# An edge network on one core: the node layer's own-row product moved into the product stage, and a hand-ordered head

## The chip, the cores and the metric

The kernel runs on one core of a Trainium2 chip. The core has a matrix engine (PE, with its weight loads shown as PEld), a vector engine (DVE), an activation engine (ACT), a general engine (POOL, GpSimd) and a queue engine (SP) that only issues transfers. Transfers are issued by SP, ACT and POOL and carried out by 16 DMA engines. Each engine works through its own list of instructions in order; semaphores tie the lists together. The metric is device time in microseconds; lower is better. The profile is one execution of the same program.

## The reference

One layer of a graph network over 12,500 nodes with 64 features and 212,500 edges, sorted by destination, with a hidden width of 128:

```
h   = relu(layernorm(x))                                  # 12500 x 64
e   = silu([h[src], h[dst], w] @ eW1 + eb1)               # 212500 x 128, eW1 is 129 x 128
e   = silu(e @ eW2 + eb2)                                 # 212500 x 128
agg = segment_sum(e, src, 12500)                          # 12500 x 128
out = x + silu([h, agg] @ nW1 + nb1) @ nW2 + nb2          # nW1 is 192 x 128, nW2 is 128 x 64
```

So the edges arrive sorted by destination, and their results must be summed by source.

## The kernel before, in words

The first edge layer is split: `h @ eW1[:64]` (table `ta`, by source) and `h @ eW1[64:128]` (table `tb`, by destination) are made once per node. Each table entry is kept as a rounded value and the rest that rounding left, two times 128 numbers.

**Head.** Constants, the source list `srcR`, the destination list `dstR`, the edge weights `ewR` and the first 16 x 128 nodes (`x0`) are loaded; `norm` normalises the nodes, `first_rows` makes a small `tb0`, and `tb00` from its first 512 nodes, so that edges can be handled before all of `tb` exists. `destinations` turns `dstR` into `rowsD`, `sources` turns a half of `srcR` into bucket (`bkt`) and place in the bucket (`locE`), `edge_weights` splits `ewR` into a rounded part and a rest and writes both to DRAM (`ews`).

**Sends.** Edges are handled in 208 blocks of 1024. For a block, `load` fetches the window of `tb` rows that its destinations need, `count` (DVE: `oh`, `each`, `pick`, `terms`, `rank`, `to`) computes the row of the scratch table `q` that each edge goes to, and `send` multiplies the window by a selection (`qp`, L493), copies it out (`qs`, ACT, L505 and L508) and scatters 128 edges with one indirect transfer on POOL (L515), eight for a block and 1,661 in all. `send_all` interleaves the pieces of `send(s)` and `count(s+1)`, three pieces for a block.

**Product stage.** A generator `feed` makes `ta` and `tb` in the pauses between pieces: for every 4 of the 100 node buckets, `products` transposes the normalised nodes (`ht`, L721), calls `product` for `ta`, stores the transposed nodes to `hd`, and calls `product` for `tb`. `product` does four matmuls (L246), two ACT copies that round (L250) and two DVE subtractions that form the rest (L253). Every `yield` in these generators is a point at which the order of issue goes over to something else.

**Steps.** The edges of a source bucket come back from `q` in 14 levels (`LEVELS`) of 25 batches; 450 steps of 512 edges do `pt`, `e1`, `p2`, `e2` and the segment sum `seg`. Which sends come between which steps is fixed when the program is written, by `PLAN_*` and `marks`. A level can be fetched (`fetch`) once its last block has been sent.

**Node layer.** In the last level each of the 25 batches is followed by `nodes`: two matmuls of `aggT` with `w1g` (L312), two of the nodes read back from `hd` with `w1n` (L315), SiLU (L317), a second product (L321), the sum with `x` (L324, `os`), and two stores on SP (L126). `nodes_in` loads `xr` (two transfers, L126 too) and the transposed nodes (L302). A flag that says whether the general path is needed is computed at the very end (L980 to L984).

The four engine lists PE, DVE, ACT and SP are in written order from the allocation of the PSUM pools on; before that a scheduler orders them. The granted clock of PE is shown in each window.

Of the kernel before, what the change touches and what calls it, by code (L numbers as in the profile page):

```python
# [28 lines left out]
F32 = mybir.dt.float32  # L29
# [10 lines left out]
P = 128  # L40
L = 125
# [38 lines left out]
def tile_gnn(ctx: ExitStack, tc: tile.TileContext, x, src, dst, ew, eW1, eb1, eW2, eb2, nW1, nb1, nW2, nb2, out):  # L80
# [11 lines left out]

    const = ctx.enter_context(tc.tile_pool(name="const", bufs=1))
# [35 lines left out]
    NE, EARLY, FIRST_PAIRS = 16, 30, 2  # L129
# [11 lines left out]
    firstR = lp.tile([P, NT], I32, name="firstR")  # L141
# [4 lines left out]
    nc.vector.memset(srcR[96:NP, LAST:], N)  # L146
    nc.vector.memset(ewR[96:NP, LAST:], 0.0)
    nc.vector.memset(firstR, 0)
    for a in range(2):
        nc.vector.memset(dstR[a * HB + HB // 2 : (a + 1) * HB, NT - 1], (2 + a) * STEP)  # L150
    ones = const.tile([1, P], F32, name="ones")
    nc.vector.memset(ones, 1.0)
    warm = const.tile([1, 1], F32, name="warm")
    nc.scalar.activation(warm, ones[:, 0:1], AF.Sqrt)
    for j0, j1 in ((0, G), (G, NE)):
        nc.sync.dma_start(x0[:, j0:j1], x[j0 * P : j1 * P, :].rearrange("(p j) d -> p j d", j=j1 - j0))
    vec = lambda v, lo_, n, m: bass.AP(tensor=v.tensor, offset=v.offset + lo_, ap=[[m, n], [1, m]])
    three = lp.tile([3, H], F32, name="three")
    three2 = lp.tile([3, 2, H], F32, name="three2")
    nc.scalar.dma_start(three[0:2, :], rows_of(eW1[2 * D : 2 * D + 1, :], 2))  # L160
    nc.scalar.dma_start(three[2:3, :], rows_of(eb1, 1))
    for to, v, queue in ((srcR, src, nc.sync), (ewR, ew, nc.scalar)):
        for p0, p1 in ((0, 96), (96, NP - 1)):
            queue.dma_start(to[p0:p1, :], vec(v, p0 * PAIR, p1 - p0, PAIR))
        queue.dma_start(to[NP - 1 : NP, :LAST], vec(v, (NP - 1) * PAIR, 1, LAST))
    shown = lambda p0, n, lo_, dims: bass.AP(tensor=dst.tensor, offset=dst.offset + p0 * PAIR + lo_, ap=[[PAIR, n]] + dims)
    MORE = LAST - BLK - HALF
    for T in range(NT):
        for a in range(2):
            whole = min(HB, NP - T * HB) - (a == 1 and T == NT - 1)  # L170
            for n0, n1 in ((0, HB // 2), (HB // 2, HB)):
                n1 = min(n1, whole)
                of = shown(T * HB + n0, n1 - n0, a * HALF, [[BLK, 2], [1, HALF]])
                nc.sync.dma_start(dstR[a * HB + n0 : a * HB + n1, T], of)
            n = min(HB, NP - T * HB)
            nc.scalar.dma_start(firstR[a * HB : a * HB + n, T : T + 1], shown(T * HB, n, 0, [[1, 1]]))
    at = HB + NP - 1 - (NT - 1) * HB
    nc.sync.dma_start(dstR[at : at + 1, NT - 1, 0], shown(NP - 1, 1, HALF, [[1, HALF]]))
    nc.sync.dma_start(dstR[at : at + 1, NT - 1, 1, :MORE], shown(NP - 1, 1, BLK + HALF, [[1, MORE]]))
    last = bass.AP(tensor=dst.tensor, offset=dst.offset + E - FEW, ap=[[PAD, 1], [0, PAD // FEW], [1, FEW]])  # L180
    nc.scalar.dma_start(dstR[at : at + 1, NT - 1, 1, MORE:].rearrange("p (r e) -> p r e", e=FEW), last)

    ident = const.tile([P, P], F32, name="ident")
    make_identity(nc, ident)
    identb = const.tile([P, P], BF16, name="identb")
    nc.vector.tensor_copy(identb, ident)
    part_i = const.tile([P, 1], I32, name="part_i")
    nc.gpsimd.iota(part_i, pattern=[[0, 1]], base=0, channel_multiplier=1)
    part = const.tile([P, 1], F32, name="part")
    nc.vector.tensor_copy(part, part_i)  # L190
    part1 = const.tile([P, 1], F32, name="part1")
    nc.vector.tensor_scalar(part1, part, 1.0, None, op0=OP.add)
    nodes_i = const.tile([P, L], I32, name="nodes_i")
    nc.gpsimd.iota(nodes_i, pattern=[[1, L]], base=1, channel_multiplier=0)
    nodes1 = const.tile([P, L], F32, name="nodes1")
    nc.vector.tensor_copy(nodes1, nodes_i)
# [4 lines left out]
    for a in range(2):  # L201
        half = slice(a * D, (a + 1) * D)
        nc.gpsimd.dma_start(w1[half, :, :], eW1[: 2 * D, :].rearrange("(s k) f -> k s f", s=2))
    same = const.tile([P, 1], F32, name="same")
# [9 lines left out]
    for extra in extras:  # L214
        nc.vector.tensor_copy(extra, plus[:, :, None].to_broadcast([P, 2, HALF]))
# [8 lines left out]
    none = const.tile([P, NB], BF16, name="none")  # L224
    nc.vector.memset(none, 0.0)
    bad = const.tile([P, 2], F32, name="bad")
    nc.vector.memset(bad, 0.0)

# [9 lines left out]
    def product(s, hr, ps, tag, to):  # L238

        abs_ = []  # L240
        for a in range(2):

            half = slice(a * D, (a + 1) * D)
            ab = ps.tile([P, G // 2, H], F32, name="ab", tag=tag)
            for i in range(G // 2):
                nc.tensor.matmul(ab[:, i], hr[half, i, :], w1[half, s, :], start=True, stop=True)  # L246
            abs_.append(ab)
# [3 lines left out]
        yield  # L251
        for a in range(2):
            nc.vector.tensor_tensor(to[:, a, 1], abs_[a], to[:, a, 0], op=OP.subtract)  # L253

    hd = dram.tile([P, NB // 2, P], F32, name="hd")
# [3 lines left out]
    NW = 3  # L259
    wins = [const.tile([P, 2, 2, 2, H], F32, name=f"win{i}") for i in range(NW)]  # L260
    sels = [const.tile([P, P], BF16, name=f"sel{i}") for i in range(NW)]
    for win in wins:
        nc.vector.memset(win, 0.0)
# [71 lines left out]
    with ExitStack() as work:  # L335
# [67 lines left out]
        def count(s):  # L403
# [37 lines left out]
            if s:  # L441
                picked()
# [677 lines left out]
```

## Time and profile before

| | us |
|---|---|
| median of 3 runs (2364.10 to 2369.81) | 2369.58 |
| the profiled execution, time | 2367.31 |
| the profiled execution, span | 2365.5 |
| first and last indirect send on POOL start | 42.16 and 2173.3 |
| busy: PE, DVE, POOL, ACT | 2028.7, 1814.7, 1655.9, 1333.0 |

Rows of the timeline have start, duration, engine, line and operation; "x8" is the number of instructions merged into the row, and the bracket is the idle time of the engine ahead of it with what ended it. Rows of the windows give the busy time of PE, PEld, DVE, ACT and POOL in a stretch, with the number of instructions, then the granted clock of PE (1.00 is full speed), the share of the DMA engines and GB/s. In the source view three durations are least, median and most, in ns.

### The profile page before, as it was taken

What the parts mean: (1) busy time and instruction counts of PE and PEld (TensorE: products, weight loads), DVE (VectorE), ACT (ScalarE), POOL (GpSimd) and SP (SyncE); (2) the same over time, 40 slices, a digit from 0 to 9 for tenths busy, and PEclk for the clock granted to TensorE, in tenths of its full rate; (3) what the DMA queues carried; (4) which work ended last, traced back from release to release, by engine and by line L of the source; (5) the groups of instructions that cost most, each with busy time, mean ns of one, the idle gap of its engine ahead of it and who ended that gap; (6) DMA issues with size and microseconds to landing.
All of it is one profiled execution on the core that took longest, in us unless ns stands there. A gap on an engine that the chain in (4) does not pass through costs nothing.

```text
span 2365.5 us, 47589 instructions
## 1 busy us (share of the span) xinstructions
PE 2028.7 (86%) x16818; PEld 1902.7 (80%) x16818; DVE 1814.7 (77%) x2865; ACT 1333.0 (56%) x2966; POOL 1655.9 (70%) x1724
## 2 busy tenths in 40 slices
PE   4667798952599779969995999999999999989997
PEld 2455697942499669959995999999999999989885
DVE  8899788885488868886886888888888888875221
ACT  3334464631277547737773777666666666656542
POOL 5777777777777777777777777777777777776110
PEclk9655597965699879979996999999999999999998
DMA  5566797964488647867884888888888888878662
GB/s 161 188 235 231 268 298 248 324 225 133 155 297 263 224 170 250 264 197 255 288 286 143 284 280 265 268 276 271 285 267 291 274 275 277 272 244 277 196 196 85
DMA packets 239835, 572.83 MB, mean 242 GB/s; under 512 B 46756, under 2 KB 99072, under 8 KB 239177
## 3 DMA queue, kind: packets, MB, share of 16 engines
q1 hardware_dynamic: 155283, 390.76, 51.5%
q0 software_dynamic: 54112, 124.65, 14.4%
q10 hardware_dynamic: 30196, 54.31, 7.3%
q8 instruction: 136, 2.23, 0.4%
q14 instruction: 108, 0.88, 0.1%
HBM read 356.61 MB, written 212.87 MB: 241 GB/s over the span
## 4 chain that ended last, share of the span: by engine, by line
PE 58%; DMA 12%; DVE 11%; POOL 6%; issue 4%; ACT 2%; SPq 2%; POOLq 0%; DVEq 0%; ACTq 0%
PE seg L675 15%; PE p L661 14%; PE pt L622 10%; DMA q<-qs,to 8%; PE pt L615 6%; POOL q L515 6%; PE qp L493 6%; PE lr L601 4%; DMA out_dram<-os 3%; DVE each L434 1%; DVE oh L426 1%; PE bc L379 1%; DVE rank L453 1%; DVE terms L451 1%; DVE pick L415 1%
## 5 line engine op out<-in xcount | busy, mean ns | idle before, releaser
L515 POOL DMA_INDIRECT q<-qs,to x1661 | 1616.1, 973 | 526.5 <-issue 396.9
L631 ACT ACTIVATE e<-pt 128x512 f32<-128x512 f32 x450 | 268.7, 597 | 496.2 <-PE pt L622 495.2
L675 PE MATMUL seg<-one,e 128*128 128x125 f32 x3600 | 502.3, 283 | 2.0 <-DVE aggT L686 1.7
L661 PE MATMUL p<-w,e 128*128 128x128 f32 x3600 | 498.6, 282 | 0.0
L661 PEld LDWEIGHTS p<-w,e 128*128 128x128 f32 x3600 | 449.9, 195 | 9.9 <-issue 9.2
L675 PEld LDWEIGHTS seg<-one,e 128*128 128x128 f32 x3600 | 444.2, 193 | 9.4 <-issue 4.9
L622 PE MATMUL pt<-oneT,a 125*128 125x128 f32 (+1 forms) x2800 | 423.0, 289 | 14.4 <-DMA a<-ta 8.5
L493 PEld LDWEIGHTS qp<-win,pick 128*128 128x128 f32 x1664 | 268.5, 224 | 202.6 <-ACT qs L505 121.6
L493 PE MATMUL qp<-win,pick 128*128 128x256 f32 x1664 | 347.7, 340 | 93.5 <-ACT qs L505 60.6
L505 ACT COPY qs<-qp 128x512 f32<-128x512 f32 x418 | 245.1, 587 | 323.9 <-DMA q<-qs,to 222.9
L622 PEld LDWEIGHTS pt<-oneT,a 125*128 125x128 f32 x2800 | 356.8, 194 | 18.3 <-issue 9.7
L644 DVE TENSOR_TENSOR one<-misc,qt 128x500 f32<-128x500 f32 x450 | 302.4, 672 | 78.1 <-PE seg L675 42.1
L686 DVE TENSOR_TENSOR aggT<-aggT,seg 128x500 f32<-128x500 f32 x325 | 218.4, 672 | 185.9 <-PE seg L675 182.2
L434 DVE TENSOR_REDUCE each<-oh 128x100 bf16<-128x800 bf16 x208 | 321.0, 1543 | 7.2
L615 PE MATMUL pt<-ident,qt 128*128 128x128 f32 x1800 | 276.3, 277 | 10.4 <-ACT qs L505 10.1
L606 ACT CAST oneT<-lr 125x512 fp32r<-125x512 f32 x450 | 265.5, 590 | 13.2 <-PE lr L601 13.2
L665 ACT ACTIVATE e<-p 128x512 f32<-128x512 f32 x450 | 268.7, 597 | 6.1 <-PE p L661 6.1
L655 ACT COPY p<-b2f 128x512 f32<-128x512 f32 x450 | 267.2, 594 | 0.0
L451 DVE TENSOR_TENSOR terms<-oh,misc 128x800 f32<-128x800 bf16 x208 | 203.6, 979 | 38.2 <-PE misc L439 38.2
L615 PEld LDWEIGHTS pt<-ident,qt 128*128 128x128 f32 x1800 | 215.3, 144 | 19.7 <-ACT qs L505 11.0
L453 DVE TENSOR_REDUCE rank<-terms 128x8 f32<-128x864 f32 x208 | 219.0, 1053 | 7.2
L426 DVE TENSOR_TENSOR oh<-misc,bkt 128x800 bf16<-128x800 f32 (+1 forms) x209 | 203.8, 975 | 2.4 <-ACT bkt L831 2.4
(153 smaller groups left out, 1653.4 us busy)
## 6 DMA issues: line engine op xcount, KB each, us to landing
a<-ta SPq DMA_DIRECT2D x350, 512.0 KB
qt<-q SPq DMA_DIRECT2D x250, 288.0 KB
qt<-q SPq DMA_DIRECT2D x100, 576.0 KB
q<-zeros ACTq DMA_DIRECT2D x25, 1080.0 KB
q<-qs,to POOLq DMA_INDIRECT x1661
win<-tb SPq DMA_DIRECT2D x208, 120.0 KB
tb<-got SPq DMA_DIRECT2D x30, 512.0 KB
q<-zeros ACTq DMA_DIRECT2D x20, 720.0 KB
```

Source lines behind the costliest of these rows:

```text
L434: nc.vector.tensor_reduce(each, oh.rearrange("p t b -> p b t"), AX.X, OP.add)
L493: nc.tensor.matmul(qp[:, t % 2, :k], halves(pick[:, t * P : (t + 1) * P]), halves(win[:, :k, v]), start=v == 0, stop=v == 1,)
L515: ins = nc.gpsimd.indirect_dma_start(out=q[:], out_offset=bass.IndirectOffsetOnAxis(ap=to[:k, j : j + 1], axis=0), in_=qs[:k, t % 2, a, :] ...
L606: nc.scalar.copy(halves(oneT), st[k].pop("lr"))
L615: nc.tensor.matmul(pt[:, t, :], qt[:, j, :H], ident, is_transpose=True, start=t == 0, stop=False, skip_group_check=True)
L622: nc.tensor.matmul(pt[:, cols, :], halves(a[:L, b, i * H : (i + 1) * H]), halves(oneT[:, cols, :]), start=False, stop=i == 1, skip_group_c ...
L631: nc.scalar.activation(e1, pt, AF.Silu)
L644: nc.vector.tensor_tensor(one.rearrange("p (b j) l -> p b j l", j=n), spots[:, None, None, :].to_broadcast(wide), loc[:, tiles[0][1] : til ...
L655: nc.scalar.copy(p2, b2f)
L661: nc.tensor.matmul(p2[:, t, :], e1[:, t, :], w2, start=False, stop=t == G - 1, skip_group_check=True)
L665: nc.scalar.activation(e2, p2, AF.Silu)
L675: nc.tensor.matmul(item[2][:, b, :], e2[:, t, :], one[:, t, :], start=j < G, stop=j >= G * (n - 1))
```

## The change

Three things are done at once.

1. **`product`.** The rest is no longer subtracted on DVE. PE multiplies the rounded copy with a negated identity (`less`) into the same PSUM tile, and ACT copies what is left. The `yield` inside `product` goes, so the calls are plain.
2. **The node layer's own rows.** `products` multiplies the transposed nodes with `w1n` at once (two matmuls `zo`, two ACT copies) and stores 128 x 500 numbers to `own` in place of 128 x 256 to `hd`. In the last level one matmul with `w1g` over 500 columns is added to what DVE has copied from `own` into a PSUM bank, and one SiLU follows. The copy for the next batch is issued right behind `os` (`then`). The last level's first fetch comes one batch later.
3. **The head.** All four lists are in written order from the start. Only 512 nodes, the first half of the destination list (by rows) and of the source list (by columns) and the first block's weights are loaded ahead of the first window; everything else goes on the SP queue behind it, the small weights too, which POOL issued before. The memsets move from DVE to POOL. `FIRST_PAIRS` is 3. All of `send(0)` comes ahead of the feed, and the feed gives nothing in the first three pieces. The flag is computed with the last block (`flagged`), and the order of the last steps is written out (`ending`).

The order of issue on PE from the first step to the last sends, 13,329 instructions, is the same in both kernels. In the product stage the old order puts 50 products into the 20 blocks 3 to 22 (blocks counted by their `bc` matmul, L379); the new one puts 48 products, 23 pairs of transposes and 24 pairs of `zo` matmuls into the 15 blocks 5 to 19, and none behind.

```diff
@@ product
             for i in range(G // 2):
-                nc.tensor.matmul(ab[:, i], hr[half, i, :], w1[half, s, :], start=True, stop=True)
+                nc.tensor.matmul(
+                    ab[:, i], hr[half, i, :], w1[half, s, :], start=i == 0, stop=False, skip_group_check=True
+                )
...
             nc.scalar.copy(halves(to[:, a, 0]), abs_[a])
-        yield
         for a in range(2):
-            nc.vector.tensor_tensor(to[:, a, 1], abs_[a], to[:, a, 0], op=OP.subtract)
+            nc.tensor.matmul(
+                abs_[a], halves(less), halves(to[:, a, 0]), start=False, stop=True, skip_group_check=True
+            )
+        for a in range(2):
+            nc.scalar.copy(halves(to[:, a, 1]), abs_[a])
@@ products
-            yield from product(0, hr, mm, "mm", rows_a)
-            nc.sync.dma_start(hd[:, b // 2 : (b + G) // 2, :], hr)
-            yield
+            product(0, hr, mm, "mm", rows_a)
+            zos = fp1.tile([P, G * L], F32, name=f"zos{b // G % 2}")
+            zo = [mm.tile([P, G // 2, L], F32, name="zo", tag="mm") for _ in range(2)]
+            for a in range(2):
+                half = slice(a * D, (a + 1) * D)
+                nc.tensor.matmul(zo[a], w1n[half, :], hr[half, :, :L], start=True, stop=True)
+            for a in range(2):
+                nc.scalar.copy(zos.rearrange("p (i a l) -> p i a l", a=2, l=L)[:, :, a], zo[a])
+            yield
+            nc.sync.dma_start(own[:, b // G, :], zos)
...
-            yield from product(1, hr, mm, "mm", got)
+            product(1, hr, mm, "mm", got)
@@ nodes, nodes_in
-        hr = sb.tile([P, G // 2, P], F32, name="hrn")
-        nc.sync.dma_start(hr, hd[:, b // 2 : b // 2 + G // 2, :])
+        zo = sb.tile([P, G * L], F32, name="zo")
+        nc.sync.dma_start(zo, own[:, B, :])
...
+        if bank is not None:
+            nc.tensor.matmul(bank, w1g, sums, start=False, stop=True, skip_group_check=True)
+            nc.scalar.activation(zsv, bank, AF.Silu, bias=nb1c)
...
         nc.vector.tensor_tensor(os_, o, xr, op=OP.add)
+        for more in then:
+            nc.vector.tensor_copy(bank, more())
         yield
@@ send_all
+                if s == 0:
+                    for _ in send(s):
+                        pass
+                for j, _ in enumerate(itertools.zip_longest(send(s) if s else (), count(s + 1))):
                     if s + 1 == nblocks and j == 1:
                         counted(s)
+                        flagged()
@@ s_pt
-                fetch(c * (NB // G) + B + NQ)
+                i = c * (NB // G) + B
+                while len(fetched) <= i + NQ and (len(fetched) < final or i + 3 >= final):
+                    fetched.append(0)
+                    fetch(len(fetched) - 1)
@@ the head
-            order = [rows_, rows_, made[0], src0, made[0], src0, weights, lists_, made[0], made[0], src0, src0, lists_]
-            order += [lists_, src0, src0]
+            order = [rows_, lists_, rows_, firstw, lists_, src0, rows_, made[0], src0, firstw, lists_, made[0], src0]
+            order += [lists_, made[0], lists_]
             for part_ in order:
                 next(part_)
+            nc.vector.tensor_copy(upto, zone)
             load(0)
             load_rows(0)
+            load(1, rows=False)
+            load_sources(1)
+            load_weights()
+            for _ in src0:
+                pass
+            for _ in count(0):
+                pass
+            load_destinations(1)
+            load_x0(G, NE)
...
             for win in wins[1:]:
-                last_rows_of(win)
+                last_rows_of(win, nc.sync)
             later_weights()
...
+            feed = itertools.chain(norm(x0[:, G:], NE - G), turns(made[1:], 2), destinations(1))
+            feed = itertools.chain(feed, itertools.islice(rest, 40), checks(), rest)
             for i, _ in enumerate(send_all(0, 2 * FIRST)):
+                if i == 0:
+                    nc.scalar.copy(halves(ewH), ewR)
-                for _ in range(2 if i < PIECES else 4):
+                for _ in range(0 if i < PIECES else 2 if i < 2 * PIECES else 4):
                     next(feed, None)
```

More of the change, by code (lines that the diff above doesn't have):

```diff
@@ L258, in tile_gnn, with last_rows_of @@
     base_i = const.tile([1, NT * HB], I32, name="base_i")
[L259 to L263, printed above, removed]
-    def last_rows_of(win):
+    def last_rows_of(win, queue):
         for a in range(2):
```

323 lines of the change are left out of this document (168 added, 155 removed).

## The prediction

> **What bounds the kernel now.** I read the page's costliest groups first, then the source view and the timeline of the scatter on POOL, then windows by stage, then the chain of waits at the end.
>
> ```profile
> span 2365.5 us, 47589 instructions
> L515 POOL DMA_INDIRECT q<-qs,to x1661 | 1616.1, 973 | 526.5 <-issue 396.9
> ```
>
> ```profile
> L515 POOL DMA_INDIRECT q<-qs,to x1661: 905/969/1905, 42.2 to 2173.3; - x185
> ```
>
> ```profile
> 42.16 1.91 POOL L515 DMA_INDIRECT q<-qs,to  x1 [10.50 <-ACT qs L508]
> ...
> 92.30 0.96 POOL L515 DMA_INDIRECT q<-qs,to  x1 [2.98 <-ACT qs L508]
> ...
> 126.13 0.96 POOL L515 DMA_INDIRECT q<-qs,to  x1 [2.73 <-ACT got L250]
> ...
> 1000.06 0.97 POOL L515 DMA_INDIRECT q<-qs,to  x1 [0.30 <-issue]
> 1001.33 0.97 POOL L515 DMA_INDIRECT q<-qs,to  x1 [0.30 <-issue]
> ```
>
> ```profile
> 78.00:240.00 162.00, 117.65 (x539) 88.44 (x537) 149.58 (x267) 63.93 (x185) 119.75 (x121) 0.51 0.64 228
> ...
> 400.00:1500.00 1100.00, 915.30 (x7724) 872.42 (x7723) 850.66 (x1298) 635.93 (x1405) 836.73 (x864) 0.88 0.72 240
> 1500.00:2174.00 674.00, 658.44 (x6046) 646.23 (x6045) 571.27 (x880) 438.43 (x959) 513.04 (x529) 1.00 0.85 274
> 2174.00:2365.00 191.00, 170.94 (x1367) 149.54 (x1365) 47.25 (x87) 85.17 (x170) 18.47 (x26) 0.97 0.55 167
> ```
>
> POOL's scatter is the pace of the whole middle. Two neighbours start 1.27 us apart (1000.06, 1001.33): 0.97 of work and 0.30 of issue. The window 400 to 1500 holds 864 of them, 1100/864 = 1.273 each; from 126.13, where the 57th starts, to 2173.3 there are 1604 intervals, 1.276 each. So POOL has no slack after 126 us: whatever delays the stream there arrives at the end in full, and whatever starts it earlier does too. Ahead of it are 42.16 us of head and, up to 126.13, stalls of 83.97 - 56 x 1.273 = 12.7 us (3.0 of them at 92.30). A block of eight sends has 8 x 1.273 = 10.2 us.
>
> In the product stage (78 to 240) PE is 73% busy at a granted clock of 0.51, and DVE is 92% busy. Behind the last send the node layer takes 191 us.
>
> ```profile
> 2229.80 0.43 DVE os L324
> 2230.25 0.32 SPq L126
> 2230.62 0.40 SPq L126
> ...
> 2232.46 3.42 DMA out_dram<-os
> 2236.09 0.44 DVE os L324
> ```
>
> This chain repeats for 18 batches at about 6.3 us: `os` frees the buffer that SP's next `xr` load waits for, SP goes on to the store of an older batch, and that store's landing frees the buffer of the next `os`. PE is not in it.
>
> **The change part by part.**
>
> The rows for the product stage:
>
> ```profile
> 210.29 0.65 PE L379 MATMUL bc<-rowsD,sel 128*128 128x512 bf16 x1
> ...
> 213.46 1.22 PE L493 MATMUL qp<-win,pick 128*128 128x256 f32 x4 [0.46 <-ACT hr L725]
> ...
> 226.17 0.37 ACT L725 COPY hr<-ht 128x256 f32<-128x256 f32 x1 [1.81 <-PE ht L721]
> 226.60 2.24 PE L246 MATMUL ab<-w,hr 64*128 64x128 f32 x16 [0.46 <-ACT hr L725]
> 227.90 0.65 ACT L250 CAST rows_a<-ab 128x256 fp32r<-128x256 f32 x2 [1.35 <-PE ab L246]
> ...
> 231.68 0.69 PE L721 MATMUL ht<-ident,xs 128*128 128x128 f32 x2 [0.22 <-ACT qs L505]
> ```
>
> ```profile
> L253 DVE TENSOR_TENSOR got<-ab,got x58: 402/415/431, 24.3 to 272.4; 128x256 f32<-128x256 f32 x58
> ...
> L253 DVE TENSOR_TENSOR rows_a<-ab,rows_a x50: 406/415/426, 70.0 to 259.2; 128x256 f32<-128x256 f32 x50
> ```
>
> ```profile
> 1702.87 0.69 PE L493 MATMUL qp<-win,pick 128*128 128x256 f32 x4
> ...
> 2201.68 0.69 PE L315 MATMUL z<-hrn,w1n 64*128 64x250 f32 x4
> ...
> 2353.48 0.37 PE L981 MATMUL fp<-ident,s 128*1 128x128 f32 x1 [0.57 <-DVE os L324]
> ...
> 2354.27 0.14 DVE L984 CAST flag_i<-m 1x1 int32<-1x1 f32 x1
> ```
>
> *Product.* DVE loses 108 x 0.415 = 45 us; that is work beside POOL, worth nothing by itself. PE gains two matmuls a product and, because they stand right behind the four and read what ACT has copied, a wait in the middle. Before, two products run back to back in 2.24, 1.12 each. After, from the start of the four: ACT begins 1.30 later (226.60 to 227.90), its first copy ends at 1.67, the first `less` starts at about 1.72; the second copy ends at 1.95, the second `less` runs 2.0 to 2.26 (a 128x256 matmul by the `qp` row is 1.22/4 = 0.30 with its tail). So 2.26 us of PE's list instead of 1.12. Bounds: 1.72 if the wait were hidden (1.12 + 2 x 0.30), 2.9 if ACT is busy with another copy pair (+0.65) whenever it is wanted. I take 2.26: nothing stands between the matmuls, and ACT has room (64 us busy in 162). ACT gains two copies of 0.37 a product.
>
> *Own rows.* Two `zo` matmuls a group have the shape of L315, 0.69 at full clock; at the half clock of this stage `qp` takes 1.22 (213.46) where it takes 0.69 at full clock (1702.87), so I take 1.15 (bounds 1.0 and 1.4) and 0.65 of ACT.
>
> *Their place.* The order now has 48 products, 24 `zo` pairs and 23 transpose pairs in 15 blocks. PE for these: base 15 x 3.5 (two `qp` of 1.22, `bc` 0.65, two small counts 0.4) = 52; 48 x 2.26 = 108; 24 x 1.15 = 28; 23 x 0.65 = 15; the `b2f` fill 4. Sum 207 us, 13.8 a block, against POOL's 15 x 10.2 = 153. With the low values 171 (base 3.1), with the high ones 252 (base 3.9). The same accounting for the old order, 20 blocks with 50 products and 25 transposes, gives 20 x 3.5 + 50 x 1.12 + 25 x 0.69 = 143 of 204 us, 70%, beside the 73% that the window shows. So in the changed kernel PE, not POOL, sets the pace of these blocks. A dense block of the old order shows it in small: 3.0 us of POOL idle at 92.30 follow four products in one block.
>
> *Head.*
>
> ```profile
> 17.73 1.03 ACT L818 CAST sf<-srcR 104x1024 f32<-104x1024 int32 x1
> ...
> 21.00 0.69 DVE L820 TENSOR_SCALAR t<-sf 104x1024 f32<-104x1024 f32 x1
> ...
> 23.18 1.23 DVE L824 SCALAR_TENSOR_TENSOR sf<-t,sf 104x1024 f32<-104x1024 f32 x1
> ...
> 31.62 0.98 DVE L426 TENSOR_TENSOR oh<-misc,bkt 128x800 bf16<-128x800 f32 x1
> 32.63 1.49 DVE L434 TENSOR_REDUCE each<-oh 128x100 bf16<-128x800 bf16 x1
> ...
> 36.65 1.05 DVE L453 TENSOR_REDUCE rank<-terms 128x8 f32<-128x864 f32 x1
> ...
> 39.06 0.75 DVE L415 SCALAR_TENSOR_TENSOR pick<-bc,same,extra 128x512 fp32r<-128x512 f32 x1 [1.16 <-DMA extra<-ewR]
> ```
>
> The first send now hangs on the source list as before, but that starts at about 11 in place of 17.7: the first nodes are a quarter (about 0.3 for each of DVE's passes, not 1.2), and the memsets and the two `extra` fills have left DVE. From 11: the cast on ACT 1.0, three passes of 0.69, one of 1.2 and the list subtraction 1.2 end at about 17; the transposes' copies on ACT, behind the first product, at 21; then `oh` 0.98, `each` 1.49, `pick` 0.75 (which waits until about 25 for the first window and its weights: store at 17.5, landed 21, load landed 24.5), `terms` 1.0, `rank` 1.05 and small ones: 28.5. So the first send starts at about 28.5 instead of 42.16 (bounds 25 and 33). Part is given back: block 2's weights now travel through DRAM behind block 1's count, and its window behind some 33 transfers on SP, which I put at about 15 us of issue; block 2 starts at about 56 where block 1 ends at 52. At block 4 I have 78 against 92.3, a gain of 14 (bounds 7 and 20). PE enters block 5 then, with no lead.
>
> *Stage end.* 78 + 207 + 1 = 286 for the first send of block 19. Before, it is 126.13 + 96 x 1.273 = 248.3. So POOL is 38 late, and nothing behind gives it back, since the order of PE from the first step to the last sends is unchanged and POOL was full there. With 171 and an entry at 72 it is 4 early, with 252 and 85 it is 90 late.
>
> *Node layer.* PE loses the two L315 pairs (0.69 a batch) and ACT half a SiLU, but the chain above has neither; its period is set by SP and the stores. The load of `own` is 256 KB where `hd` was 128, ahead of the store on the same queue: 0 to 0.7 us a batch at the 167 GB/s shown, I take 0.2, +4 over 18 batches. DVE's copy into the bank (a 128x500 pass, about 0.8 by L253's 0.415 for 256 columns) follows `os` and must end before PE's next `z`; z, SiLU, the second product and `os` are about 3.5 more, 4.4 together, under 6.3, so it costs nothing there. The flag off the end (2353.48 to 2354.41 and its read) saves 1 to 2, unless the last store, begun beside it, lands later still. Tail +2 (bounds -4 and +12). The later first fetch moves one batch's load by a step, hidden behind 3.4 us of the steps ahead of it or costing as much.
>
> Sum, against the profiled execution's 2367.3 (2.3 under the median 2369.58): + 38 + 2 = 2407.
>
> **The rivals.**
>
> *POOL stays the pace (the other side).* If a product costs PE little, only the head's gain is left, 14 to 16 us, with the tail's 2: 2353. It decides at 248.3 - 79 = 169 us for the 15 blocks, 11.3 each: a product of 1.46 and not 2.26. The way to it is the clock:
>
> ```profile
> 165.42:168.83 3.41, 3.41 (x21) 3.09 (x20) 1.90 (x4) 1.07 (x4) 2.56 (x3) 0.50 0.52 185
> 168.83:172.24 3.41, 0.32 (x2) 0.00 (x0) 3.16 (x5) 0.11 (x1) 2.74 (x3) 1.00 0.74 260
> ...
> 185.90:189.31 3.41, 3.41 (x17) 2.80 (x16) 2.83 (x7) 1.51 (x5) 2.72 (x3) 0.50 0.99 364
> ```
>
> At full clock the PE pieces shrink by 0.69/1.22 and the wait stays: a product about 1.6, the stage 48 x 1.6 + 15 x 2 + 24 x 0.69 + 23 x 0.4 + 3 = 135, under POOL's 153. A denser PE might earn it. For it: the window at 165.42, full of matmuls, is followed by one at 1.00. Against it: the window at 185.90 is as full and is followed by 0.50, a mean of 0.51 over the stage's 162 us is 162 x 0.01/0.5 = 3.2 us at full clock, one such window, and the new order puts a hole of 0.4 into every product. The Trainium skill (TensorE: Matmul & The Clock Gate, Part 1: The HAM clock gate) says that one busy window of about 3.4 us releases the clock; by that rule alone this rival would be the likely one, and the row at 185.90 differs.
>
> *Nothing to measure.* The wait is partly hidden and the tail is at its bad end: POOL 5 early to 5 late, tail -4 to +8: 2358 to 2376, about 2367. Against it: both have to fall together.
>
> **How the numbers follow.** My forecast, PE sets the pace at half clock, 0.66; its own range is 2376 to 2445, by 171 to 235 us of stage. The first rival 0.24 (2342 to 2364). The second 0.10. About 0.3% (7 us) is what a measurement of this kernel can tell from no change. Faster: 0.19 from the first rival, 0.03 from the second, 0.01 from the forecast, 0.23. Same: 0.05 + 0.05 + 0.03 = 0.13. Slower: 0.64. The range leaves out the quickest half of the first rival and the slowest tenth of the forecast: 2352 to 2432.
>
> **What would show it.** In the changed kernel: the first send at 25 to 33; block 4 at 72 to 85; between 80 and 285 idle time of POOL of 30 us or more that ends with ACT's `qs`, PE waiting for ACT's `got` and `rows_a` copies about 0.45 a product, clock near 0.5; from 300 on 1.273 a send again; the last send at about 2211; the period of `os` 6.3 to 6.9. I am wrong if the clock between 80 and 240 is near 1, or if POOL's idle time there stays under 15 us.

## The result, and the profile after

The changed kernel takes 2472.36 us (median; 2468.2 to 2481.17) where the kernel before takes 2368.40: a ratio of 1.0446 (95% interval 1.0430 to 1.0462), 104 us slower. The forecast was 2407 with a range up to 2432. The direction was right and the size was not. The profiled execution is the longest of the four, 2481.17 us, so its rows show some 9 us more than the median. Two groups of the runs below were made on chips where the kernel before itself takes 3555 and 3503 us (mean granted clock about 0.80); their ratios are given, but the accounts rest on the other groups.

The profile's page of the changed kernel, its head and the scatter's group, and then the timeline of POOL (start, duration, the idle time ahead and what ended it): the first send, the first of block 2, of block 5 and of block 19, and the last.

```profile
span 2479.4 us, 47758 instructions
...
L548 POOL DMA_INDIRECT q<-qs,to x1661 | 1615.9, 973 | 660.9 <-issue 399.7
```

```profile
29.26 1.28 POOL L548 DMA_INDIRECT q<-qs,to  x1 [15.18 <-ACT qs L541]
...
127.03 0.97 POOL L548 DMA_INDIRECT q<-qs,to  x1 [66.97 <-ACT qs L541]
...
175.47 0.96 POOL L548 DMA_INDIRECT q<-qs,to  x1 [8.12 <-ACT qs L541]
...
365.91 0.96 POOL L548 DMA_INDIRECT q<-qs,to  x1 [0.30 <-issue]
...
2289.88 0.97 POOL L548 DMA_INDIRECT q<-qs,to  x1 [0.30 <-issue]
```

POOL is as busy as before, but idle 660.9 us ahead of its sends where it was 526.5. Against the kernel before, the first send is 12.9 early. Block 2 started at 68.18 there and starts at 127.03 here, 58.9 late. Blocks 2 to 5 lose 13.7 more, blocks 5 to 19 take 190.4 where they took 147.7 (102.93 to 250.59), 42.8 more. The lateness at block 19 is then 115.3, and 116.6 at the last send. Behind it come 189.5 us where there were 192.2. So everything is lost ahead of block 19, and half of it in one hole of 67 us ahead of block 2, of which the prediction knew nothing. (A block is named by its first send: "blocks 5 to 19" runs from the first send of block 5 to that of block 19, 14 blocks, for which POOL alone needs 143 us.)

The timeline of the queues in that hole (ACT's queue issues the stores of the split weights, SP's queue fills the last rows of the windows), and two windows inside it (busy time of PE, PEld, DVE, ACT and POOL, the granted clock, the share of the DMA engines, GB/s):

```profile
40.15 0.22 ACTq L900 DMA_DIRECT2D ews<-ewH  x1
43.78 8.21 ACTq L900 DMA_DIRECT2D ews<-ewR  x1
```

```profile
35.30 0.78 SPq L302 DMA_DIRECT2D win<-three  x1
...
75.30 2.71 SPq L302 DMA_DIRECT2D win<-three  x3
...
106.87 2.69 SPq L302 DMA_DIRECT2D win<-three  x4
...
118.62 0.75 DVE L441 SCALAR_TENSOR_TENSOR pick<-bc,same,extra 128x512 fp32r<-128x512 f32 x1 [64.49 <-DMA extra<-ews]
```

```profile
60.00:75.00 15.00, 0.00 (x0) 0.00 (x0) 0.00 (x0) 0.00 (x0) 0.06 (x1) 1.00 0.08 31
79.00:106.00 27.00, 0.00 (x0) 0.00 (x0) 0.00 (x0) 0.00 (x0) 0.00 (x0) 1.00 0.06 27
```

```profile
SPq L302 <- DMA ews<-ewH: 39.2, 1, 39.2
SPq L302 <- DMA ews<-ewR: 28.8, 1, 28.8
```

In both windows the engines do next to nothing. In the second the DMA engines together are busy 6% of the time, which is one of sixteen, and move 27 GB/s. Two stores of 103 rows, 824 KB each, stand behind each other: 1.69 MB at 27 GB/s is 62 us. `pick` of block 2 waits 64.49 us for the weights that it reads back from them. The last view, the waits of SP's queue (us in total, times, longest), shows that SP's small transfers to the windows stood still for the same two stores, although they take nothing from them. Block 2's own window and weights stand behind them in SP's list: SP goes on at 106.87 and issues the load of the weights at 116.17.

### The profile page after: what moved, and what is told of

It is laid out like the page before. It is cut to its first block, busy times and chain, and to the rows that moved or that the text cites. A ratio compares the mean times of both kernels' runs of the same rounds, so it can differ in the third digit from the quotient of the medians.

```text
span 2479.4 us, 47758 instructions
## 1 busy us (share of the span) xinstructions
PE 2067.4 (83%) x16880; PEld 1929.5 (78%) x16880; DVE 1792.0 (72%) x2785; ACT 1382.7 (56%) x3107; POOL 1647.4 (66%) x1714
## 5 line engine op out<-in xcount | busy, mean ns | idle before, releaser
L548 POOL DMA_INDIRECT q<-qs,to x1661 | 1615.9, 973 | 660.9 <-issue 399.7
L685 DVE TENSOR_TENSOR one<-misc,qt 128x500 f32<-128x500 f32 x425 | 285.9, 673 | 79.0 <-PE seg L716 43.9
L441 DVE SCALAR_TENSOR_TENSOR pick<-bc,same,extra 128x512 fp32r<-128x512 f32 x208 | 154.6, 743 | 114.0 <-DMA extra<-ews 65.2
L653 PEld LDWEIGHTS pt<-ident,qt 128*128 128x128 f32 x1800 | 215.9, 144 | 20.8 <-ACT qs L538 12.3
```

Source lines behind the costliest of these rows:

```text
L548: ins = nc.gpsimd.indirect_dma_start(out=q[:], out_offset=bass.IndirectOffsetOnAxis(ap=to[:k, j : j + 1], axis=0), in_=qs[:k, t % 2, a, :] ...
L653: nc.tensor.matmul(pt[:, t, :], qt[:, j, :H], ident, is_transpose=True, start=t == 0, stop=False, skip_group_check=True)
L685: nc.vector.tensor_tensor(one.rearrange("p (b j) l -> p b j l", j=n), (spots if c < len(LEVELS) - 1 else nodes1)[:, None, None, :].to_broa ...
```

## The experiments

Ratios are to the kernel before, run beside each kernel on the same chip.

**The store.** Three kernels. The first cuts the store into 96 and 7 rows:

```diff
-                nc.scalar.dma_start(ews[i, 1:], v[1:].rearrange("p (g a e) -> p g a e", g=2, a=2))
+                for p0, p1 in ((1, 97), (97, NP)):
+                    nc.scalar.dma_start(ews[i, p0:p1], v[p0:p1].rearrange("p (g a e) -> p g a e", g=2, a=2))
```

> The changed kernel, with the store of the split edge weights to DRAM cut into 96 and 7 rows in place of one piece of 103 rows; nothing else. Theory S (the store): the two pieces of 103 rows run on one DMA engine, 31 us each one behind the other, and hold both the SP queue and block 2's weights back. Then block 2 starts at 56 to 60 and not at 127, and the time falls by some 70 us from 2472 to about 2400 (2392 to 2412). Theory Q (the SP queue's order: last window rows and small weights stand ahead of block 2's loads): the store hardly matters, block 2 starts after 100, 2440 to 2472. Theory P (the product stage paces anyway and takes the time back): block 5 earlier by 70, block 19 hardly, about 2460.

The second leaves the 103 rows whole and issues them on POOL's queue (`nc.gpsimd` for `nc.scalar`):

> The changed kernel, with the same two stores of 103 rows issued on POOL's queue in place of ACT's. If 103 rows cannot be spread over engines whatever the queue, the time stays 2465 to 2480 and the DMA share stays near 6% for some 60 us. If it is the hardware queue that does not spread them, the time is that of the cut into 96 and 7 rows, about 2400 plus the 1.1 us that POOL spends on two issues.

The third is the kernel before, with `ews[i, 1:]` stored on ACT's queue where it stored `ews[i]`, 104 rows, on POOL's:

> The kernel before, with only the store of the split weights changed: rows 1 to 103 on ACT's queue in place of rows 0 to 103 on POOL's. Theory S: it is issued at about 30 and lands at about 94 in place of about 40, block 2 starts near 105 in place of 68, and since POOL has no slack the time is 2368 + 37 = 2405 (2395 to 2425). Theory Q or a hidden store: 2364 to 2375.

Measured: 2410.06 (ratio 1.0178, 1.0161 to 1.0195), 2410.32 (1.0187, 1.0161 to 1.0212) and, for the kernel before with the long store, 2415.28 (1.0189, 1.0172 to 1.0206). All three times agree with theory S. The store alone costs the changed kernel 1.0446 - 1.0178 = 0.027, 63 us, and costs the kernel before 45, where block 2 starts at 113.05, 44.9 late. Of the first kernel the timeline of POOL (block 2, block 19, the last send), the issue and the window of its store, SP's list behind it, and of the second kernel one of SP's waits:

```profile
69.42 0.97 POOL L548 DMA_INDIRECT q<-qs,to  x1 [13.21 <-ACT qs L541]
...
289.60 0.97 POOL L548 DMA_INDIRECT q<-qs,to  x1 [0.30 <-issue]
...
2216.33 0.97 POOL L548 DMA_INDIRECT q<-qs,to  x1 [0.30 <-issue]
```

```profile
40.12 0.69 ACTq L901 DMA_DIRECT2D ews<-ewH  x2
```

```profile
40.00:48.00 8.00, 1.86 (x8) 1.24 (x7) 7.82 (x9) 0.73 (x2) 5.22 (x5) 1.00 0.78 239
```

```profile
44.66 7.11 SPq L302 DMA_DIRECT2D win<-three  x8
51.82 0.64 SPq L317 DMA_DIRECT2D b2f<-in_L_gnn_eb_dram  x1
...
57.48 1.02 SPq L424 DMA_DIRECT2D win<-tb  x2
58.54 1.58 SPq L397 DMA_DIRECT2D extra<-ews  x4
```

```profile
SPq L397 <- DMA ews<-ewR: 5.3, 1, 5.3
```

Theory S was wrong in one point: block 2 starts at 69.42 and not at 56 to 60. What is left is theory Q, the order of SP's list. There the fills of the windows start at 44.66, after a wait of 9.3 us for the shortened store; the small weights follow, then block 2's window at 57.48 and its weights at 58.54, and neither of these two waits for the store. With the store on POOL's queue the fills start at 35.57, the weights are loaded at 55.12, after the wait of 5.3 us shown last, and block 2 starts at 65.48.

The window that holds the cut store has the engines 78% busy. The rows alone are not at fault, and neither is ACT's queue alone: 103 rows on POOL's queue are as good as 96 and 7 on ACT's. The Trainium skill (DMA: Bandwidth & Descriptors, Why a DMA increments its semaphore by 16 and not by 1) has the rule: a transfer issued by SP or ACT is split over the largest number up to 16 that divides the sizes of its outermost dimensions, and a transfer of GpSimd may be split in uneven shares. 103 is prime, so one engine. The traces agree with both halves: 0.06 of the engines and 27 GB/s for 103 rows on ACT's queue, 0.78 with 96 and 7 rows, and 0.46 and 0.53 in the windows 40 to 50 and 50 to 60 with 103 rows on POOL's.

In the kernel before with the long store, the first send itself is late, and SP's waits say why:

```profile
70.83 1.89 POOL L515 DMA_INDIRECT q<-qs,to  x1 [41.20 <-ACT qs L508]
```

```profile
SPq L743 <- DMA ews<-ewR: 32.9, 1, 32.9
...
SPq L368 <- DMA ews<-ewH: 17.0, 1, 17.0
```

Line 368 loads block 0's weights out of `ewH` in SBUF. It takes nothing from the store that it waited for. With the store on POOL's queue, SP's fills of the windows show no such wait. What ties the queues of SP and ACT together (a completion semaphore that both use would do it) was not tried.

**The product stage.** Two edits, each with and without the other, all with the store cut. One puts the pause of the feed back:

```diff
             nc.scalar.copy(halves(to[:, a, 0]), abs_[a])
+        yield
         for a in range(2):
             nc.tensor.matmul(
...
-            product(0, hr, mm, "mm", rows_a)
+            yield from product(0, hr, mm, "mm", rows_a)
```

The other puts the subtraction back on DVE in place of the two `less` matmuls and the second copies:

```diff
+            nc.vector.tensor_tensor(to[:, a, 1], abs_[a], to[:, a, 0], op=OP.subtract)
```

DVE with the pause:

> The changed kernel with the store cut into 96 and 7 rows, and with the rest of a product subtracted on DVE as before, with the pause of the feed inside the product. Forecast's mechanism (PE waiting for ACT's copies sets the pace of the product stage): POOL paces again at 10.2 us a block, the head's gain stays, block 19 starts at 225 to 245 in place of 250.6 and the time is about 2353 (2345 to 2362). Rival (the own rows' product alone, or the denser order, makes PE the pace): block 19 starts after 260 and the time is 2375 to 2400.

PE with the pause, and DVE without it, first on the chip where the kernel before takes 3555 us (ratios 1.0064, 1.0039 to 1.0089, and 1.0078, 1.0048 to 1.0108) and then again:

> The changed kernel, store cut into 96 and 7 rows, and the pause of the feed back inside the product, between ACT's rounding copies and the two negated matmuls; the rest of a product still made by PE and ACT. Theory W (PE loses time by waiting for ACT's copies, 0.45 to 0.5 a product): other PE work now stands in that place, the wait goes, and the time falls from 2410 by 15 to 20 to 2390 to 2397. Theory B (it is PE's busy time and the density that count): the same work is done somewhat later, 2403 to 2412.

> The changed kernel, store cut, rest subtracted on DVE, but without the pause, so that the feed is as dense as in the change (products in the blocks up to 19). Theory W: PE has 15 x 3.5 + 48 x 1.12 + 28 + 15 + 4 = 153 us for 15 blocks, POOL's pace; block 5 to block 19 takes 153 to 160 in place of 174.7 with the product on PE, nothing is left for the blocks 20 to 24, and the time is 2385 to 2392. If DVE becomes the pace instead (45 us more of it in 15 blocks), block 5 to 19 takes 165 or more and the time is 2395 to 2410.

> The same kernel as the earlier run with the pause back inside the product (PE and ACT make the rest, store cut), on another chip. Theory W (PE loses by waiting for ACT's copies): other PE work stands in that place, 2410 falls to 2390 to 2397, as low as the run with DVE's subtraction and the pause (2395). Theory B (PE's busy time and the density count, not the wait): 2403 to 2412.

> The same kernel as the earlier run with DVE's subtraction and no pause (store cut), on another chip. Theory W: 153 us of PE for 15 blocks, nothing left for the blocks 20 to 24: 2385 to 2392. If the density itself costs (DVE, PE and ACT in turn holding each other up): 2395 to 2410.

| rest of a product made by | without the pause | with the pause |
|---|---|---|
| PE and ACT | 2410.06 (1.0178) | 2379.96 (1.0051, 1.0032 to 1.0071) |
| DVE | 2410.60 (1.0195, 1.0180 to 1.0211) | 2395.11 (1.0100, 1.0082 to 1.0118) |

Of these four, PE without the pause and DVE with it ran on one chip, the other two on another; the ratios make them comparable.

Waits in the window 105 to 345 (us in total, times, longest), which reaches past the last product of all four (309.9), in this order: PE's in the kernel with PE and no pause, PE's with PE and the pause, DVE's with DVE and no pause, DVE's with DVE and the pause:

```profile
PE ab L287 <- ACT got L285: 14.9, 23, 3.3
PE ab L287 <- ACT rows_a L285: 10.8, 22, 0.5
```

```profile
PE ab L288 <- ACT rows_a L285: 8.6, 9, 4.0
...
PE ab L288 <- ACT got L285: 3.1, 6, 0.7
```

```profile
DVE got L285 <- ACT got L283: 20.9, 15, 3.3
DVE rows_a L285 <- ACT rows_a L283: 10.6, 5, 5.5
```

```profile
DVE got L286 <- ACT got L283: 18.0, 7, 5.6
DVE rows_a L286 <- ACT rows_a L283: 10.6, 7, 2.8
```

DVE with the pause was expected at 2353 by the forecast's mechanism and came at 2395: the product on PE was not the whole of it. The pause is worth 1.0178 - 1.0051 = 0.013, 30 us, with PE, more than the 15 to 20 that theory W gave it, and 1.0195 - 1.0100 = 0.0095, 22 us, with DVE. In the profiled executions it brings block 24, which lies behind the last product in all of them, forward by 15.2 us with PE (340.75 to 325.56) and by 19.3 with DVE (345.33 to 326.08).

The traces account for the gain only with PE. Without the pause PE stands right behind ACT's copies and waits 25.7 us for them; with it 11.7. These 14.0 us are nearly the 15.2. DVE's wait hardly changes, 31.5 and 28.6, so where its gain comes from stays open. Blocks 5 to 19 take 174.7 us in the kernel with PE and no pause and 152.6 with the pause, but part of that is only put off: about 43 products run there without the pause and 36 with it, and the rest meets the blocks behind.

So theory B falls for PE (2380 against 2403 to 2412), and so does the part of theory W that charged PE's extra matmuls: DVE without the pause is no faster than PE without it. With the pause the medians put the product on PE 1.0100 - 1.0051 = 0.005, 12 us, ahead. The traces do not bear this out: block 24 starts at 325.56 with PE and at 326.08 with DVE, and 7.9 of the 12.7 us between the two profiled executions lie behind the last send, where both run the same code. That the product is cheaper on PE is not shown.

**The own rows and the head.** DVE with the pause, the own rows undone (`hd`, two pairs of `z` matmuls and two SiLUs as before), which leaves the new head alone:

```diff
-            zo = [mm.tile([P, G // 2, L], F32, name="zo", tag="mm") for _ in range(2)]
...
-            nc.sync.dma_start(own[:, b // G, :], zos)
+            nc.sync.dma_start(hd[:, b // 2 : (b + G) // 2, :], hr)
```

and the same with the weights of the blocks 0 to 5 split and stored first, and the small weights loaded later:

```diff
-    nc.scalar.dma_start(ew0, bass.AP(tensor=ew.tensor, offset=ew.offset, ap=[[HALF, 4], [1, HALF]]))
+    nc.scalar.dma_start(ew0, bass.AP(tensor=ew.tensor, offset=ew.offset, ap=[[HALF, 12], [1, HALF]]))
...
-                for p0, p1 in ((1, 97), (97, NP)):
+                for p0, p1 in ((3, 99), (99, NP)):
...
             load(1, rows=False)
+            load_rows(2)
...
+                if i == 2 * PIECES:
+                    later_weights()
```

> The kernel before with the new head alone: store cut, product on DVE with its pause, and the own rows undone (transposed nodes stored, the node layer's two pairs of matmuls and two SiLUs as before). Theory O (the own rows' matmuls and copies in the product stage cost what they save and more): the 45.8 us of the blocks 20 to 23 go back to 40.8 and the 17.3 of block 7 shrinks; from block 2, which starts at 69 as before, the stream is that of the kernel before: 2366 to 2374. If the own rows are innocent there and the new order of the feed costs it, 2385 to 2396.

> As the run with the new head alone, and besides block 2 to 5's split weights go the way of block 0's (12 rows of 512 loaded, split and stored first), and the small weights are loaded two blocks later. Then block 2 no longer waits for the big store: it starts behind block 1 at 52 to 56 in place of 69. If POOL is the pace from there, the gain of 13 is kept: 2353 to 2360. If PE or DVE, full in the blocks 3 to 22, take it back, 2364 to 2372.

On the chip of 3555 us the ratios were 1.0031 (1.0005 to 1.0056) and 0.9995 (0.9966 to 1.0023). Again, on another chip:

> The same kernel as the earlier run with the new head alone (own rows undone, product on DVE with its pause, store cut), once more, since the kernel before itself took 3555 us on that chip. Expected as there: theory O (the own rows' work in the product stage costs what it saves and more) 2366 to 2374, since block 2 starts at 69 as before and nothing else is changed behind it; own rows innocent: 2385 to 2396.

> The same kernel as the earlier run whose blocks 2 to 5 get their split weights early, once more for the same reason. Block 2 started there at 58.6 against 69.2, and block 12 at 196.9 against 204.6, with everything slower. If POOL is the pace from block 2, 10 to 13 of the head's gain are kept and the time is 2353 to 2360; if PE or DVE, full in the blocks 3 to 22, take it back, 2364 to 2372.

Measured 2374.75 (1.0027, 1.0017 to 1.0036), 0.75 above theory O's range and far from its rival's, and 2364.83 (0.9986, 0.9977 to 0.9996). The own rows cost 1.0100 - 1.0027 = 0.007, 17 us, beside DVE's subtraction; at block 24 it is 12.0 (326.08 to 314.10). The new head, its store mended, is 6 us slower than the old one: the 13 us of the first send are gone by block 2, which starts at 68.29 where it started at 68.18. Two holes remain behind it. Of the kernel with the new head alone, the timeline of POOL at block 8 and of PE ahead of it, and of POOL at the blocks 22 and 23:

```profile
143.18 0.97 POOL L539 DMA_INDIRECT q<-qs,to  x1 [7.24 <-ACT qs L532]
```

```profile
136.17 2.07 PE L958 MATMUL p<-b2f,ones 1*128 1x512 f32 x2
138.91 2.07 PE L958 MATMUL p<-b2f,ones 1*128 1x512 f32 x2 [0.67 <-ACT b2f L959]
```

```profile
287.61 0.96 POOL L539 DMA_INDIRECT q<-qs,to  x1 [1.21 <-ACT qs L532]
...
296.66 0.96 POOL L539 DMA_INDIRECT q<-qs,to  x1 [4.27 <-ACT qs L532]
...
303.80 1.09 POOL L539 DMA_INDIRECT q<-qs,to  x1 [2.36 <-ACT qs L532]
```

The bank fill, which the old head had ahead of the first send, now stands between block 7 and block 8, and POOL is idle for 7.2 us there. The prediction gave it 4 us of PE. Block 22 takes 16.2 us in place of 10.2; the feed's last product starts at 296.6 there, behind the first steps (below, with the feed brought forward, block 22 takes 10.2 again). In the second kernel block 2 starts at 58.43, 9.8 earlier than in the kernel before. Its edit moves both the weights and the small loads that stood ahead of block 2's window in SP's list, and which of the two gave it was not separated. The last send is at 2174.91, after 2173.32 in the kernel before, since the two holes took the gain back.

**The tail.** The kernel before, with `("nd", 3)` in place of `("nd", 2)` for the node layer's tiles:

> The kernel before with three buffers in place of two for the node layer's tiles, nothing else. If the chain shown for the tail (store landed, os, next load, store) is what sets its period, 18 batches gain 0.4 to 0.9 each: 2351 to 2361. If SP or PE sets it: 2365 to 2371. This prices what the own-row change could at most have won in the tail.

Measured 2358.06 (0.9969, 0.9957 to 0.9981). The timeline of DVE in its tail:

```profile
2280.71 0.42 DVE L324 TENSOR_TENSOR os<-o,xr 125x256 f32<-125x256 f32 x1 [3.50 <-issue]
2286.61 0.42 DVE L324 TENSOR_TENSOR os<-o,xr 125x256 f32<-125x256 f32 x1 [3.50 <-issue]
```

The period is 5.90, where the first 17 batches of the kernel before have 6.41 on the mean, and the tail 2356.1 - 2171.46 = 184.6 in place of 192.2. In the kernel before, 18 of the 25 `os` wait for the landing of a store, 84.3 us in all; here two do, 6.9 us. So the store's landing did set the period. The own-row change left that chain alone: its tail still has

```profile
2409.00 0.42 DVE L358 TENSOR_TENSOR os<-o,xr 125x256 f32<-125x256 f32 x1 [3.93 <-DMA out_dram<-os]
2415.52 0.42 DVE L358 TENSOR_TENSOR os<-o,xr 125x256 f32<-125x256 f32 x1 [4.35 <-DMA out_dram<-os]
```

a period of 6.5 here, and 6.38 as the mean of the 16 from 2326.07 to 2428.14, beside the 6.41 before.

**Put together.** First the early weights, the bank filled while block 2 is counted, four steps of the feed a piece in the blocks 8 to 11, and three buffers:

> The kernel of the run whose blocks 2 to 5 get their weights early (2365), and three things more: the row of b2f loaded ahead on ACT's queue and the bank filled while block 2 is counted (it cost a hole of 7 us between block 7 and 8), four steps of the feed a piece in the blocks 8 to 11 in place of three (a hole of 5 us at block 22 came from its rest), and three buffers in place of two for the node layer's tiles (its store frees the buffer of the next os but one). Stream: last send at 2163 to 2169 in place of 2174.9. Tail: if the store's landing sets the period, 6.3 becomes 5.4 to 5.9 and the tail 174 to 184 in place of 189.4; if SP's order sets it, 187 to 190. Sum 2340 to 2355, or 2354 to 2360.

Measured 2355.11 (0.9962, 0.9949 to 0.9976), at the upper end of what was expected. The last send, at 2171.35, misses its 2163 to 2169 and is only 3.6 earlier than with the early weights alone: the fill now stands ahead of block 1, and block 2 starts at 63.39 in place of 58.43. The holes at the blocks 8 and 22 are smaller or gone (12.1 and 10.2 us a block). The tail fell to 179.3, as expected. Then three kernels on the chip where the kernel before takes 3503 us: the product on PE with the pause in the kernel before, and all parts mended, without and with the own rows (`b2f` now comes to all partitions by one transfer, and its banks are opened by two bf16 matmuls while PE is idle):

```diff
+    nc.scalar.dma_start(b2f, bass.AP(tensor=eb2.tensor, offset=eb2.offset, ap=[[0, P], [0, G], [1, H]]))
...
-                nc.tensor.matmul(p2, ones, b2f[0:1], start=True, stop=True)
-                nc.scalar.copy(b2f, p2)
```

> The kernel before with the rest of a product made by PE and ACT, the pause of the feed kept; nothing else. The order there is POOL's from block 7 on, so a cheaper or dearer product shows only in the 12.7 us of stalls ahead of it: 2358 to 2369 if the product on PE with its pause is no dearer than DVE's subtraction (as 2380 against 2395 says), 2372 to 2385 if PE's extra 0.6 to 1.1 us a product makes it the pace.

> New head, own rows undone, rest of a product on PE and ACT with the pause, weights of the blocks 0 to 5 first, b2f brought to all partitions by one transfer and its banks opened while PE is idle, three node-layer buffers. If the parts add up (2375 with the new head alone, -10 for the early weights, -7 for the bank, -7 for the buffers, -5 to -15 for the product): 2335 to 2346. If PE becomes the pace in the blocks 3 to 24 without DVE's help: 2350 to 2362.

> The same with the own rows' product in the product stage, as in the change: this kernel is the change with its store, its pause, its early weights, its bank and its buffers mended. If the own rows cost 20 us there whoever makes the rest of a product (2395 against 2375): 2355 to 2366. If their price came only from DVE and PE holding each other up: 2335 to 2350.

Ratios 1.0054 (1.0023 to 1.0086), 0.9960 (0.9936 to 0.9984) and 0.9989 (0.9962 to 1.0015). There the product on PE is a loss in the kernel before, and the own rows cost 0.003, with intervals that overlap. The sends are not the pace of the middle there: the window 400 to 1500 of the mended kernel holds 582 of them, and 865 in the run below. So neither ratio carries over, and whether the product on PE gains in the old head on the other chips, and what the own rows cost in the mended kernel there, stays open. The mended kernel without the own rows, again:

> The same kernel as the run that puts the mended parts together without the own rows, once more, since the kernel before took 3503 us on that chip. If the parts add up: 2335 to 2346 against 2366 to 2370. If PE becomes the pace in the blocks 3 to 24: 2350 to 2362.

Measured 2347.68 (0.9931, 0.9918 to 0.9945), 16 us faster than the kernel before and the best of the case. The timeline of POOL (first send, block 2, block 19, last send):

```profile
30.10 1.28 POOL L550 DMA_INDIRECT q<-qs,to  x1 [16.04 <-ACT qs L543]
...
59.52 0.97 POOL L550 DMA_INDIRECT q<-qs,to  x1 [2.44 <-ACT qs L543]
...
245.70 0.97 POOL L550 DMA_INDIRECT q<-qs,to  x1 [0.30 <-ACT hr L768]
...
2165.27 0.96 POOL L550 DMA_INDIRECT q<-qs,to  x1 [0.30 <-issue]
```

Of the 20.8 us between the two profiled executions (the medians lie 16 to 17 apart), 8.1 come from the stream and 12.8 from the tail (179.4 in place of 192.2). The measured 2347.68 lies 1.7 above the upper end of what the parts were expected to add up to.

## Why the prediction was wrong

The kernels undo one part after the other. The table gives what each step takes off, by the ratios (0.001 is 2.37 us) and by the start of block 24 in the profiled executions (416.93, 340.75, 325.56, 326.08, 314.10 and, for the kernel before, 301.53):

| part | by the medians, us | at block 24, us |
|---|---|---|
| the store | 63 | 76.2 |
| the missing pause, with PE | 30 | 15.2 |
| the product on PE, with its pause | -12 | -0.5 |
| the own rows | 17 | 12.0 |
| the head with its store mended | 6 | 12.6 |
| sum | 104 | 115.4 |

This is one order of undoing, with one profiled execution for each kernel, up to 9 us off its median. The store is by far the largest part in both columns; a part of some 10 us or less is not settled.

*The step that failed: the head.* The first send was forecast at 28.5 and came at 29.26. The next sentence failed: "block 2's weights now travel through DRAM behind block 1's count, and its window behind some 33 transfers on SP, which I put at about 15 us of issue; block 2 starts at about 56". It counted the issues and gave the landing of the store no price. The store is part of the change, moved to another queue and one row shorter. SP's fills of the windows alone, a part of those 15 us, took 74 (35.3 to 109.6), and block 2 started at 127. At block 4 the sum has 78, and it is 154.90. Even with the store cut block 2 starts at 69.4, because its window and weights come last in SP's list.

*Stage end.* The stage itself was forecast well: the 15 blocks 4 to 18 at 207 us, and they take 211.0 in the changed kernel. Nearly all of the miss at block 19, 365.91 for 286, is there at block 4. With the store cut the forecast time comes out too, 2410 for 2407, but partly by luck: block 4 is at 96.88, 19 late, and the 15 blocks take 192.7, 14 less than forecast. The sum also starts from 248.3 for block 19 of the kernel before, which the trace has at 250.59, so by its own terms it was 2 too high.

*Product.* Its wait is there. Of the changed kernel the timeline of PE shows one product without other work:

```profile
347.31 1.23 PE L279 MATMUL ab<-w,hr 64*128 64x128 f32 x8
...
349.04 0.86 PE L287 MATMUL ab<-got,less 128*128 128x256 f32 x2 [0.49 <-ACT got L285]
...
349.82 1.23 PE L279 MATMUL ab<-w,hr 64*128 64x128 f32 x8
```

From one product's start to the next are 2.51 us, forecast 2.26, and the wait 0.49, forecast about 0.45. That PE would set the pace was right. The cause was only half right. The prediction charged PE's matmuls and called DVE's lost 45 us worth nothing. The four kernels show that the removed pause is what costs, on either engine, and that without it the engine that makes the rest makes no difference. What the move off DVE is worth with the pause stays open.

*Own rows.* The forecast put 28 us of PE into the stage and gave the price of the stage as a whole. Their own share is 12 to 17 us. The tail was forecast at +2 and is -2.7; the reading that its chain has none of the removed work was right.

*The rivals.* POOL as the pace would have needed the clock or the pause. By the duration of four `qp` matmuls (next section), 3 of 30 rows in the blocks 5 to 19 of the changed kernel ran at full speed (under 0.9 us). With the store cut it was 13 of 31, and the blocks still took 174.7 us and not 143: a good part of this rival's clock was there and did not make POOL the pace. Why these two executions differ in speed was not tried. In the best kernel, with the pause and without the own rows, the blocks 5 to 19 take 145.9 us, so there POOL does hold the pace. The second rival, nothing to measure, fell with the first result.

## What to carry to other kernels

Price a moved store by its landing: look at the rows of its outermost dimension on the queue that now issues it, and at who reads it back. In an order written by hand, a pause between a producer's copy and its consumer can be worth more than the instructions around it (here 15 to 30 us); take it away only if nothing else could have stood there. Check a small gain of a median in the trace: if it does not lie where the change acts, it is not shown. A gain at the first instruction is kept only as far as the next thing that was late anyway.

## What was not expected of the hardware

A store of 103 rows on ACT's queue moved 27 GB/s on one engine's share (0.06); with the same store on POOL's queue the windows show 0.46 and 0.53. SP's transfers stood still for it though they take nothing from it, 39.2 and 28.8 us in the changed kernel, and still 9.3 us with 96 and 7 rows.

The clock column did not follow the speed of the matmuls. The changed kernel's window 155 to 192 shows a granted clock of 1.00, while four `qp` matmuls in it take 1.22, the duration of the half clock. In the kernel with DVE and the pause four take 0.74 at 69.91. In the kernel with the new head alone the column reads 1.00 for all of 78 to 240 (the last row), while 28 of the 29 `qp` rows of four between 105 and 256 take 1.1 or more:

```profile
155.00:192.00 37.00, 31.53 (x144) 23.06 (x142) 18.63 (x27) 20.20 (x61) 15.50 (x17) 1.00 0.62 219
```

```profile
173.09 1.22 PE L526 MATMUL qp<-win,pick 128*128 128x256 f32 x4
```

```profile
69.91 0.74 PE L521 MATMUL qp<-win,pick 128*128 128x256 f32 x4 [0.64 <-ACT hr L764]
```

```profile
78.00:240.00 162.00, 114.72 (x504) 83.63 (x506) 147.69 (x263) 62.79 (x179) 114.77 (x117) 1.00 0.59 210
```

So the prediction's sign "wrong if the clock between 80 and 240 is near 1" was a bad one: the column has 0.88 there in the changed kernel, it reads 1.00 even where PE does nothing (60 to 75), and of 16 such `qp` rows only one is at full speed. The duration of a known matmul is the surer reading.
